# Values computed once, in pass 1, with the matmuls of the scores, in a gated cross-attention layer

## The chip, the cores and the metric

The kernel runs on one core of a Trainium2 chip. The metric is the device time of one execution in microseconds. Three runs of the kernel before gave 2297.72, 2296.51 and 2291.89 us; the median is 2296.51 us. Everything is in fp32.

## The reference

The layer takes tokens x (64 batches of 128 tokens with 512 features) and a context of the same shape. It has an attention part, whose score matrix is summed over all 64 batches, and a feed-forward part.

```
xn = layernorm(x)                                  # (64, 128, 512)
Q, K, V = xn, ctx, ctx, each head times Wh[h]      # 4 heads of 128
A = max(|sum over b of (Q K^T)[b] * decay / sqrt(128)|, 1)   # (4, 128, 128)
O = A V                                            # per batch and head
Y = layernorm(O, eps=1e-3) * gamma + beta
x = x + tanh(g_xattn) * ((relu(xn @ wg) * Y) @ wo)
x = x + tanh(g_ffn) * ffn(layernorm(x))            # SwiGLU, 512 -> 1408 -> 512
```

Because A needs the sum over all batches, no batch can be finished before all batches have gone through the scores. The kernel therefore makes two passes over the data. Q K^T is computed as (xn Wh Wh^T) ctx^T, so that K itself is never needed; V = ctx Wh is.

## The kernel before

The 64 batches are handled as 16 groups of 4 batches (512 tokens). On TensorE the stationary operand is a 128x128 block, the moving operand has 128 to 512 columns, and results go to PSUM. Three PSUM buffers (the pool `ps_mm`, L98) are shared by short-lived results: the transposes `pt`, the queries `pq`, the values `pv` and the attention outputs `po`. Five more PSUM tiles have fixed names (`bank_a`, `bank_f`, `bank_b`, `bank_c0`, `bank_c1`).

**Pass 1** loops over the groups. `prepare` (L407) normalises the tokens of a group on VectorE (statistics at L171, the normalisation at L199) and transposes them on TensorE (L178), with the copy out of PSUM on VectorE (L423) or ScalarE (L425) in turn. For the group before it, `scores` (L428) makes queries with four matmuls of 512 columns (L432, copied out by ScalarE at L436) and then, for each batch and head, one matmul of 128 columns with the context as stationary operand (L442). These accumulate over all batches and groups in `bank_c1`, so pass 1 writes no score out of PSUM. `project` (L452) computes relu(xn @ wg) by a Strassen-like scheme with seven products of four 256-column matmuls each (`product`, L202, matmul at L207), evacuated by ScalarE and VectorE, and stores the result in DRAM (`w_scr`, two stores a group on ScalarE's DMA queue, L482). Beside this, `prepare_weights` loads the raw FFN and output weights, forms their block sums on GpSimd and stores them in DRAM scratch (L367 loads, L391 stores), one part for each group.

**Between the passes**, the accumulated scores are multiplied by the decay mask on VectorE (L511), made absolute on ScalarE and raised to at least 1 on VectorE, which gives `attn`.

**Pass 2** loops over the groups again. `retention` (L527) loads nothing itself: it gets the four context tiles of the group, makes the values `v` with 16 matmuls of 128 columns (L534, four head blocks for each batch, copied out by ScalarE at L538), multiplies them by `attn` (L544), normalises and transposes the result (through DRAM, `sq_scr`, for all groups but the first), and multiplies it into the gate `w_t`, which was loaded from `w_scr` at L523. `attended` (L608) multiplies by wo and adds to the tokens. `ffn` (L732) then runs on the group with Strassen-like products against weights streamed from DRAM (`gu` at L723, `dn_w` at L729). The function `interleave` (L30) mixes the steps of `ffn` of one group with those of `attended` and `retention` of the next two by their announced numbers of steps (`RET_STEPS`, `ATT_STEPS`, `FFN_STEPS`).

What decides the order: every engine runs its own instructions in program order, and so does each DMA queue. The written order above is the start; the framework reorders it when the kernel is built and puts semaphore waits where a tile is reused or where a DMA takes over one of eight DMA semaphores (so that a DMA also waits for one issued some eight places before it, from whichever queue). SP's queue carries almost all loads: the tokens `x_t` (L110, five buffers of half a group each), the context `c_t` (L119, five buffers of one batch each), the weights, and the stores of `gu_scr` and `dn_scr`.

Of the kernel before, what the change touches and what calls it, by code (L numbers as in the profile page):

```python
# [10 lines left out]
F32 = mybir.dt.float32  # L11
# [30 lines left out]
def after(steps, gen):  # L42

    for _ in range(steps):
        yield
    yield from gen
# [3 lines left out]
def flamingo_gated_layer(  # L50
# [42 lines left out]
    xin = ctx.enter_context(tc.tile_pool(name="xin", bufs=5))  # L93
    cin = ctx.enter_context(tc.tile_pool(name="cin", bufs=5))
    att = ctx.enter_context(tc.tile_pool(name="att", bufs=1))
# [20 lines left out]

    def load_ctx(b):
        t = cin.tile([P, H, S], F32, tag="c", name="c_t")
        nc.sync.dma_start(out=t, in_=ctxT[b])  # L119
        return t  # L120

# [8 lines left out]
    attn = const.tile([P, H, S], F32, name="attn")  # L130
    wh_sb = const.tile([P, H, P], F32, name="wh_sb")
    gamma_sb = const.tile([P, NC], F32, name="gamma_sb")
# [13 lines left out]
    ]  # L146
    w_scr = dram.tile([NG, 2, P, 2, TOK], F32, name="w_scr")


# [5 lines left out]
    bank_c1 = ps_bank.tile([P, TOK], F32, name="bank_c1")  # L155
    for seeded in (bank_b, bank_c0):
        for i in range(TOK // P):
            nc.tensor.matmul(
                seeded[:, i * P : (i + 1) * P], lhsT=ident, rhs=ident,
                start=(i == 0), stop=True, skip_group_check=True,  # L160
            )
# [91 lines left out]
    pass1 = ExitStack()  # L253
    rows = pass1.enter_context(tc.tile_pool(name="rows", bufs=6))
    once = pass1.enter_context(tc.tile_pool(name="once", bufs=1))
# [11 lines left out]
    x_next.append(load_x(1))  # L267
    c_next = [load_ctx(b) for b in range(GB)]
    gates = const.tile([P, 2], F32, name="gates")
# [25 lines left out]
    def constants():  # L295

        nc.sync.dma_start(out=ds, in_=down_s.partition_broadcast(P))
        nc.sync.dma_start(out=decay, in_=decayT)
        nc.sync.dma_start(out=wh_sb, in_=wh.rearrange("h d e -> d h e"))
# [104 lines left out]

    acc = bank_c1.rearrange("p (h s) -> p h s", h=H)

    def prepare(g, x_t, xnT):  # L407
# [19 lines left out]

    def scores(g, c_t, xnT):  # L428
        qs = []
        for h in range(H):  # L430
            pq = ps_mm.tile([P, TOK], F32, tag="mm", name="pq")
            nc.tensor.matmul(  # L432
                pq, lhsT=gram[:, h, :], rhs=xnT[:, h, :], start=True, stop=True
            )
            q = rows.tile([P, TOK], F32, tag="row", name="q")
            nc.scalar.copy(q, pq)  # L436
            qs.append(q)
            if h % 2:
                yield
        for j in range(GB):  # L440
            for h in range(H):
                nc.tensor.matmul(  # L442
                    acc[:, h, :],
                    lhsT=c_t[j][:, h, :],
                    rhs=qs[h][:, j * S : (j + 1) * S],
                    start=(g == 0 and j == 0 and h == 0),
                    stop=(g == NG - 1 and j == GB - 1),
                    skip_group_check=True,
                )
            yield  # L450

    def project(g, xnT):  # L452
# [34 lines left out]
    for g in range(NG):  # L487
        x_t, c_t = x_next.pop(0), c_next
# [9 lines left out]
        interleave(  # L498
            (prep, GB),
            (scores(*pending) if pending else None, 2 + GB),  # L500
            (project(pending[0], pending[2]) if pending else None, 7),
        )
        x_next.append(load_x((g + 2) % NG))
        c_next = [load_ctx((g + 1) % NG * GB + j) for j in range(GB)]
        pending = (g, c_t, xnT)
    for _ in weights:
# [3 lines left out]

    nc.vector.tensor_mul(attn, acc, decay)  # L511
    absd = rows.tile([P, H, S], F32, tag="row", name="absd")
    nc.scalar.activation(absd, attn, AF.Abs)
# [12 lines left out]

    def retention(g, c_t, ws):  # L527

        helper = nc.vector if g < 3 else nc.gpsimd
        v = att.tile([P, H, GB, P], F32, tag="v", name="v")  # L530
        for j in range(GB):
            pv = ps_mm.tile([P, H, P], F32, tag="mm", name="pv")
            for h in range(H):
                nc.tensor.matmul(  # L534
                    pv[:, h, :], lhsT=c_t[j][:, h, :], rhs=wh_sb[:, h, :],
                    start=True, stop=True,
                )
            nc.scalar.copy(v[:, :, j, :], pv)  # L538
            yield

# [11 lines left out]
        if g:  # L552
            sq = att.tile([P, NQ, NC, GB, SQ], F32, tag="v", name="sq")
        ons = []
# [53 lines left out]
    def attended(g, x_t, ws, x1nT):  # L608
# [55 lines left out]
        if g:  # L664
            sq = att.tile([P, NQ, NC, GB, SQ], F32, tag="v", name="sq")
        for j in range(GB):
# [18 lines left out]
    WAIT = 5  # L685
    RET_STEPS = 8 + WAIT + 2
    ATT_STEPS = 8 + GB

    def new_x1nT():
        return wide.tile([P, NQ, NC, GB, SQ], F32, tag="xT", name="x1nT")  # L690

    x_t, c_t = x_next.pop(0), c_next
    c_next = [load_ctx(GB + j) for j in range(GB)]
    ws = load_gate(0)
    interleave(
        (retention(0, c_t, ws), 12), (after(6, project(pending[0], pending[2])), 16),
    )
# [219 lines left out]
    def next_retention(g):  # L917

        nonlocal c_next, ws
        c_t = c_next  # L920
        ws = load_gate(g)
        yield from retention(g, c_t, ws)
        if g + 1 < NG:
            c_next = [load_ctx((g + 1) * GB + j) for j in range(GB)]
# [6 lines left out]
    interleave((attended(0, x_t, ws, x1nT), ATT_STEPS), (islice(second, 7), 10))  # L931
    pending = (0, x_t, x1nT, combine_tokens(nc.vector, x1nT))
    for g in range(NG - 1):
# [6 lines left out]
        if g == 0:  # L940
            steps.append(late_attended(1, x_t, x1nT))
            n_steps += RET_STEPS - 7
        if g + 2 < NG:
# [64 lines left out]
```

## Time and profile before

The profiled execution took 2293.72 us; its span, from the first to the last instruction, is 2291.9 us. The TensorE clock was granted at 0.999.

| what | value |
|---|---|
| median of three runs | 2296.51 us |
| profiled execution / its span | 2293.72 / 2291.9 us |
| pass 1, last scores matmul | at 350 us |
| first FFN product | at 394.6 us |
| DMA, whole span | 459.17 MB, 200 GB/s |
| DMA share in pass 1, first slices | 0.8 and falling to 0.6 |
| context loads (L119) | 128 of 256 KB, 4.3 us to landing (median) |
| token loads in pass 1 (L110) | 512 KB, 5.4 us to landing (median), 3.8 to 9.6 |
| gate stores w_scr (L482) | 32 of 512 KB on ScalarE's queue, 0.34 us to issue |
| stores of FFN sums gu_scr (L391) | 7.3 to 11.3 us to landing, median 9.7 |

How to read it: a line of a group gives the line of the code, the engine, the operation with output and input tiles, the number of instructions, their busy time and mean duration, and the idle time of the engine just before them with what ended it. PEld is the load of stationary operands; it overlaps the matmuls (PE). "SPq" and "ACTq" are DMA issues on the queues of SP and ScalarE. Lines of a timeline begin with the start in the span and the time that the merged instructions took.

### The profile page before, as it was taken

The page shows a single profiled execution, that of the slowest core. Times are in us where ns is not written, and L with a number is a line of the kernel's source. Part 1 is how long each engine was busy: PE and PEld are TensorE (multiplying, and loading weights), DVE is VectorE, ACT ScalarE, POOL GpSimd, SP SyncE. Part 2 cuts the span into 40 slices and gives each one's busy share as a digit, 9 for nine tenths or more (in the row PEclk, how much of TensorE's full clock was granted, in tenths as well). Part 3 has the DMA queues.
Part 4 walks back from the last instruction along what each step waited for, and adds up shares of the span by engine and source line. Part 5 has one row for each costly group of instructions (what it writes and reads, how often), then busy time and mean ns, then how long its engine had stood idle before and what let it go on. Part 6 is the DMA issues. An engine that isn't in the chain of part 4 may idle for free. (4 is left out here: it accounts for less than half of the span.)

```text
span 2291.9 us, 28061 instructions
## 1 busy us (share of the span) xinstructions
PE 2263.7 (99%) x10808; PEld 1945.1 (85%) x10808; DVE 861.6 (38%) x1771; ACT 574.7 (25%) x1052; POOL 674.5 (29%) x811
## 2 busy tenths in 40 slices
PE   8999999999999999999999999999999999999999
PEld 7777787888888888888888888888888888888888
DVE  6444534544333333323333423343433333333222
ACT  2333333312222221213131212121222122222221
POOL 4232202322232323232424232423223242323210
PEclk9999999999999999999999999999999999999999
DMA  8777746566565656665666656565657475645541
GB/s 266 264 232 244 248 161 228 189 195 225 178 226 173 219 187 212 197 220 193 218 197 197 208 191 225 181 214 181 214 171 236 158 236 174 230 155 186 167 149 65
DMA packets 158213, 459.17 MB, mean 200 GB/s; under 512 B 16768, under 2 KB 36864, under 8 KB 143360
## 3 DMA queue, kind: packets, MB, share of 16 engines
q1 hardware_dynamic: 152656, 440.34, 58.9%
q10 hardware_dynamic: 5424, 17.04, 1.8%
q8 instruction: 85, 1.39, 0.3%
q14 instruction: 48, 0.39, 0.1%
HBM read 376.72 MB, written 80.61 MB: 200 GB/s over the span
## 5 line engine op out<-in xcount | busy, mean ns | idle before, releaser
L207 PE MATMUL bank_c<-tcomb,gu 128*128 128x256 f32 x1920 | 456.9, 379 | 1.0 <-ACT bank_b L766 0.7
L207 PEld LDWEIGHTS bank_c<-tcomb,gu 128*128 128x128 f32 x1920 | 361.3, 190 | 49.4 <-ACT bank_b L766 1.5
L207 PE MATMUL bank_a<-x1nT,gu 128*128 128x256 f32 x1280 | 302.8, 379 | 1.1 <-ACT x1nT L677 0.7
L207 PEld LDWEIGHTS bank_a<-x1nT,gu 128*128 128x128 f32 x1280 | 242.1, 190 | 34.5 <-ACT x1nT L677 1.2
L247 POOL TENSOR_TENSOR hs<-h,h 128x256 f32<-128x256 f32 x80 | 58.0, 726 | 582.7 <-DVE h L746 582.7
L167 POOL TENSOR_TENSOR rs<-ve,mhalf 128x1 f32<-128x1 f32 x128 | 72.6, 576 | 486.4 <-DVE ve L166 471.2
L745 ACT ACTIVATE sil<-c,gs_sb 128x256 f32<-128x256 f32 x160 | 81.2, 508 | 322.7 <-DVE c L775 183.2
L603 POOL TENSOR_TENSOR w_t<-w_t,yT 128x256 f32<-128x256 f32 x112 | 77.9, 726 | 264.2 <-ACT yT L594 264.2
L207 PE MATMUL bank_b<-x1nT,gu 128*128 128x256 f32 x640 | 151.7, 379 | 0.0
L207 PE MATMUL bank_f<-tcomb,gu 128*128 128x256 f32 x640 | 151.2, 379 | 0.0
L798 PE MATMUL bank_c<-dn_w,hs 128*128 128x256 f32 x640 | 145.0, 382 | 0.0
L775 DVE TENSOR_TENSOR c<-bank_c,m 128x512 f32<-128x512 f32 x80 | 55.0, 688 | 237.6 <-PE bank_c L207 234.2
L798 PE MATMUL bank_f<-dn_w,h 128*128 128x256 f32 x640 | 143.4, 379 | 0.0
L798 PEld LDWEIGHTS bank_f<-dn_w,h 128*128 128x128 f32 x640 | 121.5, 190 | 22.4 <-issue 6.7
L207 PEld LDWEIGHTS bank_b<-x1nT,gu 128*128 128x128 f32 x640 | 121.6, 190 | 22.1 <-issue 6.2
L798 PEld LDWEIGHTS bank_c<-dn_w,hs 128*128 128x128 f32 x640 | 120.3, 190 | 19.7 <-ACT bank_b L875 4.0
L207 PEld LDWEIGHTS bank_f<-tcomb,gu 128*128 128x128 f32 x640 | 121.6, 190 | 16.6
L746 DVE SCALAR_TENSOR_TENSOR h<-bank_a,us_sb,sil 128x256 f32<-128x256 f32 x80 | 38.6, 482 | 240.2 <-ACT sil L745 240.2
L171 DVE BATCH_NORM_STATS2 st<-x_t 128x6 f32<-128x512 f32 x128 | 83.0, 684 | 103.3 <-DMA x_t<-in_x_dram 102.2
L758 ACT COPY bank_c<-bank_a 128x512 f32<-128x512 f32 x80 | 45.6, 570 | 258.6 <-PE bank_a L207 256.8
L746 DVE SCALAR_TENSOR_TENSOR h<-c,us_sb,sil 128x256 f32<-128x256 f32 x160 | 78.3, 489 | 75.1 <-ACT sil L745 75.1
L207 PE MATMUL bank_c<-t,wgc 128*128 128x256 f32 x384 | 92.5, 383 | 0.0
(166 smaller groups left out, 3518.1 us busy)
## 6 DMA issues: line engine op xcount, KB each, us to landing
gu<-gu_scr SPq DMA_DIRECT2D x80, 1024.0 KB, 4.9
dn_w<-dn_scr SPq DMA_DIRECT2D x112, 640.0 KB, 5.1
gu<-gu_scr SPq DMA_DIRECT2D x80, 768.0 KB, 5.9
c_t<-in_ctxT_dram SPq DMA_DIRECT2D x128, 256.0 KB, 4.3
x_t<-in_x_dram SPq DMA_DIRECT2D x62, 512.0 KB, 4.6
sq_scr<-sq SPq DMA_DIRECT2D x30, 1024.0 KB, 4.8
wo_w<-wo_scr SPq DMA_DIRECT2D x112, 256.0 KB, 3.9
w_scr<-w ACTq DMA_DIRECT2D x32, 512.0 KB, 5.8
```

What stands on the lines that cost most here:

```text
L167: nc.gpsimd.tensor_tensor(dst, ve, mhalf[:, :n], ALU.pow)
L171: nc.vector.bn_stats(st, src)
L207: nc.tensor.matmul(out, lhsT=w[:, s, k, :], rhs=x_k, start=(start and s == 0 and k == 0), stop=(s == 1 and k == KC - 1), skip_group_check= ...
L247: engine.tensor_tensor(s[0], a21, a22, ALU.add)
L603: (helper if d else nc.gpsimd).tensor_tensor(w, w, yT[:, :, d * KC + k, q * 2 : q * 2 + 2, :], ALU.mult)
L745: nc.scalar.activation(sil, src[:, 0:n], AF.Silu, scale=gs_sb[:, i : i + 1])
L746: nc.vector.scalar_tensor_tensor(dst, src[:, n : 2 * n], us_sb[:, i : i + 1], sil, ALU.mult, ALU.mult)
L758: nc.scalar.copy(bank_c, bank_a)
L775: nc.vector.tensor_add(c22, bank_c, m5)
L798: nc.tensor.matmul(bank[:, i * HN : (i + 1) * HN], lhsT=lhs[:, j, i * P : (i + 1) * P], rhs=dn[:, j, :], start=(start and i == 0 and j == ...
```

## The change

The values are made in pass 1. For each context block (batch j, head h) one matmul now has 256 moving columns: 128 of queries and 128 of the head matrix Wh[h]. Both lie in one tile `qw` (five slots for each head: four batches of queries and Wh in the fifth), so the moving operand is two pieces of 128 columns with a step between them. Two batches share one PSUM tile `sv` of the pool `ps_mm`: the scores of both accumulate in its first part, the values go to the second and third. After each `sv` tile, VectorE adds the scores to `attn` in SBUF (the first time it copies them), and ScalarE copies the values into `v`. A group's `v` (1 MB) is stored in DRAM (`v_scr`) by ScalarE's queue, and pass 2 loads it back with one load on SP's queue in place of the four context loads. From the second group on, the context of pass 1 is loaded by ScalarE's queue, issued after the scores of the group before. Pass 2 no longer reads the context.

`bank_c1` no longer holds the scores and is seeded with the other banks at the start; the transposition buffer `sq` of pass 2 no longer shares its place with `v`; the pools of context and queries end with pass 1. `retention` is four steps shorter, and the first group's `project` starts three steps before `retention` does.

```diff
-    def load_ctx(b):
-        t = cin.tile([P, H, S], F32, tag="c", name="c_t")
-        nc.sync.dma_start(out=t, in_=ctxT[b])
-        return t
+    def load_ctx(g, engine):
+        tiles = []
+        for j in range(GB):
+            t = cin.tile([P, H, S], F32, tag="c", name="c_t")
+            engine.dma_start(out=t, in_=ctxT[g * GB + j])
+            tiles.append(t)
+        return tiles
...
-    for seeded in (bank_b, bank_c0):
+    for seeded in (bank_b, bank_c0, bank_c1):
...
+    qw = once.tile([P, H, GB + 1, P], F32, name="qw")
+    nc.sync.dma_start(out=qw[:, :, GB, :], in_=wh.rearrange("h d e -> d h e"))
...
-    def scores(g, c_t, xnT):
-        qs = []
+    def scores(g, xnT):
+        nonlocal c_next
+        c_t = c_next
         for h in range(H):
-            pq = ps_mm.tile([P, TOK], F32, tag="mm", name="pq")
+            pq = ps_mm.tile([P, GB, S], F32, tag="mm", name="pq")
             nc.tensor.matmul(
                 pq, lhsT=gram[:, h, :], rhs=xnT[:, h, :], start=True, stop=True
             )
-            q = rows.tile([P, TOK], F32, tag="row", name="q")
-            nc.scalar.copy(q, pq)
-            qs.append(q)
+            nc.scalar.copy(qw[:, h, 0:GB, :], pq)
             if h % 2:
                 yield
-        for j in range(GB):
-            for h in range(H):
-                nc.tensor.matmul(
-                    acc[:, h, :],
-                    lhsT=c_t[j][:, h, :],
-                    rhs=qs[h][:, j * S : (j + 1) * S],
-                    start=(g == 0 and j == 0 and h == 0),
-                    stop=(g == NG - 1 and j == GB - 1),
-                    skip_group_check=True,
-                )
-            yield
+        v = att.tile([P, H, GB, P], F32, tag="sq" if g % 2 else "v", name="v")
+        for h in range(H):
+            for q in range(2):
+                sv = ps_mm.tile([P, 4, P], F32, tag="mm", name="sv")
+                for i in range(2):
+                    j = 2 * q + i
+                    nc.tensor.matmul(
+                        sv[:, 0 : 2 + i : 1 + i, :],
+                        lhsT=c_t[j][:, h, :],
+                        rhs=qw[:, h, j : GB + 1 : GB - j, :],
+                        start=(i == 0),
+                        stop=(i == 1),
+                        skip_group_check=True,
+                    )
+                if g == 0 and q == 0:
+                    nc.vector.tensor_copy(attn[:, h, :], sv[:, 0, :])
+                else:
+                    nc.vector.tensor_add(attn[:, h, :], attn[:, h, :], sv[:, 0, :])
+                nc.scalar.copy(v[:, h, 2 * q : 2 * q + 2, :], sv[:, 1:3, :])
+            yield
+        nc.scalar.dma_start(out=v_scr[g], in_=v)
+        if g + 1 < NG:
+            c_next = load_ctx(g + 1, nc.scalar)
...
-    nc.vector.tensor_mul(attn, acc, decay)
+    nc.vector.tensor_mul(attn, attn, decay)
...
+    def load_values(g):
+        v = att.tile([P, H, GB, P], F32, tag="v", name="v")
+        nc.sync.dma_start(out=v, in_=v_scr[g])
+        return v
+
-    def retention(g, c_t, ws):
+    def retention(g, v, ws):
...
-        v = att.tile([P, H, GB, P], F32, tag="v", name="v")
-        for j in range(GB):
-            pv = ps_mm.tile([P, H, P], F32, tag="mm", name="pv")
-            for h in range(H):
-                nc.tensor.matmul(
-                    pv[:, h, :], lhsT=c_t[j][:, h, :], rhs=wh_sb[:, h, :],
-                    start=True, stop=True,
-                )
-            nc.scalar.copy(v[:, :, j, :], pv)
-            yield
...
-            sq = att.tile([P, NQ, NC, GB, SQ], F32, tag="v", name="sq")
+            sq = att.tile([P, NQ, NC, GB, SQ], F32, tag="sq", name="sq")
...
-    RET_STEPS = 8 + WAIT + 2
+    RET_STEPS = 4 + WAIT + 2
...
-        (retention(0, c_t, ws), 12), (after(6, project(pending[0], pending[2])), 16),
+        (after(3, retention(0, v, ws)), 11), (project(*pending), 9),
```

More of the change, by code (lines that the diff above doesn't have):

```diff
@@ L93, in flamingo_gated_layer @@
     xin = ctx.enter_context(tc.tile_pool(name="xin", bufs=5))
-    cin = ctx.enter_context(tc.tile_pool(name="cin", bufs=5))
     att = ctx.enter_context(tc.tile_pool(name="att", bufs=1))
@@ L130, in flamingo_gated_layer @@
     attn = const.tile([P, H, S], F32, name="attn")
-    wh_sb = const.tile([P, H, P], F32, name="wh_sb")
     gamma_sb = const.tile([P, NC], F32, name="gamma_sb")
@@ L147, in flamingo_gated_layer @@
     w_scr = dram.tile([NG, 2, P, 2, TOK], F32, name="w_scr")
+    v_scr = dram.tile([NG, P, H, GB, P], F32, name="v_scr")
     bank_a = ps_bank.tile([P, TOK], F32, name="bank_a")
@@ L253, in flamingo_gated_layer @@
     pass1 = ExitStack()
-    rows = pass1.enter_context(tc.tile_pool(name="rows", bufs=6))
+    cin = pass1.enter_context(tc.tile_pool(name="cin", bufs=5))
     once = pass1.enter_context(tc.tile_pool(name="once", bufs=1))
@@ L267, in flamingo_gated_layer @@
     x_next.append(load_x(1))
-    c_next = [load_ctx(b) for b in range(GB)]
+    c_next = load_ctx(0, nc.sync)
+    qw = once.tile([P, H, GB + 1, P], F32, name="qw")
+    nc.sync.dma_start(out=qw[:, :, GB, :], in_=wh.rearrange("h d e -> d h e"))
     gates = const.tile([P, 2], F32, name="gates")
@@ L298, in constants @@
         nc.sync.dma_start(out=decay, in_=decayT)
-        nc.sync.dma_start(out=wh_sb, in_=wh.rearrange("h d e -> d h e"))
         nc.sync.dma_start(out=gamma_sb, in_=gamma.rearrange("(c p) -> p c", p=P))
@@ L403, in rest_weights @@
         )
-    acc = bank_c1.rearrange("p (h s) -> p h s", h=H)
     def prepare(g, x_t, xnT):
@@ L487, in flamingo_gated_layer @@
     for g in range(NG):
-        x_t, c_t = x_next.pop(0), c_next
+        x_t = x_next.pop(0)
         xnT = wide.tile([P, NC, TOK], F32, tag="xT", name="xnT")
@@ L499, in flamingo_gated_layer @@
             (prep, GB),
-            (scores(*pending) if pending else None, 2 + GB),
-            (project(pending[0], pending[2]) if pending else None, 7),
+            (scores(*pending) if pending else None, 2 + H),
+            (project(*pending) if pending else None, 7),
         )
         x_next.append(load_x((g + 2) % NG))
-        c_next = [load_ctx((g + 1) % NG * GB + j) for j in range(GB)]
-        pending = (g, c_t, xnT)
+        pending = (g, xnT)
     for _ in weights:
@@ L508, in flamingo_gated_layer @@
     interleave((scores(*pending), 1))
-    nc.vector.tensor_mul(attn, acc, decay)
-    absd = rows.tile([P, H, S], F32, tag="row", name="absd")
+    nc.vector.tensor_mul(attn, attn, decay)
+    absd = once.tile([P, H, S], F32, tag="m5p", name="absd")
     nc.scalar.activation(absd, attn, AF.Abs)
@@ L664, in attended @@
         if g:
-            sq = att.tile([P, NQ, NC, GB, SQ], F32, tag="v", name="sq")
+            sq = att.tile([P, NQ, NC, GB, SQ], F32, tag="sq", name="sq")
         for j in range(GB):
@@ L690, in new_x1nT @@
         return wide.tile([P, NQ, NC, GB, SQ], F32, tag="xT", name="x1nT")
-    x_t, c_t = x_next.pop(0), c_next
-    c_next = [load_ctx(GB + j) for j in range(GB)]
+    x_t = x_next.pop(0)
+    v = load_values(0)
     ws = load_gate(0)
     interleave(
-        (retention(0, c_t, ws), 12), (after(6, project(pending[0], pending[2])), 16),
+        (after(3, retention(0, v, ws)), 11), (project(*pending), 9),
     )
@@ L917, in next_retention @@
     def next_retention(g):
-        nonlocal c_next, ws
-        c_t = c_next
+        nonlocal ws
+        v = load_values(g)
         ws = load_gate(g)
-        yield from retention(g, c_t, ws)
-        if g + 1 < NG:
-            c_next = [load_ctx((g + 1) * GB + j) for j in range(GB)]
+        yield from retention(g, v, ws)
     def late_attended(g, x_t, x1nT):
@@ L930, in flamingo_gated_layer @@
     second = next_retention(1)
-    interleave((attended(0, x_t, ws, x1nT), ATT_STEPS), (islice(second, 7), 10))
+    interleave((attended(0, x_t, ws, x1nT), ATT_STEPS), (islice(second, 4), 8))
     pending = (0, x_t, x1nT, combine_tokens(nc.vector, x1nT))
@@ L941, in flamingo_gated_layer @@
             steps.append(late_attended(1, x_t, x1nT))
-            n_steps += RET_STEPS - 7
+            n_steps += RET_STEPS - 4
         if g + 2 < NG:
```

## The prediction

> **What bounds the kernel now.** I read part 1 of the page first, then the busy time by stage, then single groups in order of time.
>
> ```profile
> PE 2263.7 (99%) x10808; PEld 1945.1 (85%) x10808; DVE 861.6 (38%) x1771; ACT 574.7 (25%) x1052; POOL 674.5 (29%) x811
> ```
>
> TensorE is the bound. The stage table (span; then busy time of PE, PEld, DVE, ACT, POOL; clock; DMA share; GB/s) shows where it still waits:
>
> ```profile
> 100.00:200.00 100.00, 96.47 (x507) 78.66 (x506) 47.94 (x102) 34.77 (x57) 27.06 (x25) 1.00 0.72 245
> 200.00:300.00 100.00, 95.10 (x518) 79.27 (x517) 44.01 (x91) 32.03 (x52) 21.60 (x19) 1.00 0.68 229
> 600.00:700.00 100.00, 100.00 (x464) 87.07 (x463) 36.48 (x78) 21.41 (x40) 34.63 (x43) 1.00 0.62 203
> ```
>
> Pass 2 is solid matmul; pass 1 (to about 350 us) loses 4 to 5%. Two groups of instructions are touched by the change, and one shows the waits of pass 1 (last field: idle time before, by releaser):
>
> ```profile
> L534 PE MATMUL pv<-wh_sb,c_t 128*128 128x128 f32 x512 | 67.5, 275 | 0.0
> L442 PE MATMUL bank_c<-q,c_t 128*128 128x128 f32 x512 | 67.3, 275 | 0.0
> L432 PE MATMUL pq<-xnT,gram 128*128 128x512 f32 x128 | 62.0, 608 | 12.3 <-DVE xnT L423 9.4 <-DVE mean_var L172 2.9
> ```
>
> Each fp32 matmul is two passes (256 matmuls, x512). Their 275 ns overlap, so the pace must be read from starts. One group of pass 1, TensorE:
>
> ```profile
> 102.13 1.89 PE L207 MATMUL bank_a<-xnT,wgc 128*128 128x256 f32 x8
> ...
> 120.45 1.06 PE L442 MATMUL bank_c<-q,c_t 128*128 128x128 f32 x8
> 121.34 1.89 PE L207 MATMUL bank_c<-t,wgc 128*128 128x256 f32 x8
> 123.07 1.89 PE L207 MATMUL bank_a<-xnT,wgc 128*128 128x256 f32 x8
> 127.32 1.10 PE L432 MATMUL pq<-xnT,gram 128*128 128x512 f32 x2 [2.36 <-DVE xnT L423]
> ```
>
> A pass of 128 columns takes 0.89/8 = 0.111 us, one of 256 takes 1.73/8 = 0.216 us; a group takes 123.07 - 102.13 = 20.94 us. The 2.36 us stall is explained by SP's queue and VectorE in the same group:
>
> ```profile
> 103.38 0.96 SPq L391 DMA_DIRECT2D gu_scr<-gu_raw  x2
> 113.89 1.92 SPq L367 DMA_DIRECT2D gu_raw<-in_gateT_dram  x4
> ...
> 118.44 0.41 SPq L110 DMA_DIRECT2D x_t<-in_x_dram  x1
> ```
>
> ```profile
> 124.50 1.29 DVE L171 BATCH_NORM_STATS2 st<-x_t 128x6 f32<-128x512 f32 x2 [6.14 <-DMA x_t<-in_x_dram]
> ```
>
> Five groups out of sixteen look like this: the raw FFN weights wait until the last store of sums has landed, the tokens queue behind them, and VectorE, which runs in order, stands 6.14 us at the statistics. Today little hangs on VectorE at that point.
>
> **The arithmetic on TensorE.** Removed: 512 + 512 passes of 128 columns, 1024 x 0.111 = 113.7 us. Added: 256 matmuls of 256 columns, 512 x 0.216 = 110.6 us. Gain 3.1 us. The strided moving operand is charged nothing: products on x1nT, cut into 4x2x32, also run at 379 ns a pass. Here the Trainium skill would promise more. "TensorE: Matmul & The Clock Gate", section "LDWEIGHTS (loading the stationary operand)", gives a load of 128 columns as columns/1.2 ns, 107 ns, and the change saves 512 loads: 55 us if they stood in the way. The pace of 0.111 us a pass with a load in each says that they overlap the streaming, so I take 3.1. The eight seeding matmuls of bank_c1 lie in the wait for the first tokens: nothing.
>
> Work moves, too: a group of pass 1 grows from 20.94 to 20.94 - 32 x 0.111 + 32 x 0.216 = 24.3 us, and pass 2 loses 3.6 us a group.
>
> **Pass 2.** Four context loads of 256 KB become one v load of 1 MB, 4.9 us to landing by the gu row of that size. In the built order it is issued as soon as the previous group's po matmuls have read v, a whole FFN ahead (119 us between like products of two groups), so it costs nothing; so do the ScalarE copies that go (ACT is 21% busy). With sq in a buffer of its own nothing waits for v longer.
>
> **What pass 1 gets: 8 evacuations a group.** Each sv tile needs a VectorE addition of 128x128 (estimate 0.38 us, from 0.48 at 256 and 0.69 at 512 elements) and then a ScalarE copy of 128x256 (0.47 us, what L745 takes from bank_c). In the built order the copy waits for the addition, and TensorE's tile three further on waits for the copy (three PSUM buffers, shared with pq and pt). The busy time is covered: 8 x 0.38 = 3 us and 8 x 0.47 = 3.8 us in 24 us on engines that are half idle or more. What is not covered is standing in line. I count from G, the start of a group's first product on TensorE: product 1.73, two pq 1.72, pt 0.44, product 1.73, half product 0.86, two pq 1.72, half product 0.86, pt 0.44 make 9.5; two sv tiles 11.2; product 12.95; two sv 14.7; product 16.4; pt and one sv 17.7. The next sv needs the buffer of the tile finished at 14.7. But the built order of VectorE puts the two statistics of the next tokens between the additions of the two tiles finished before 14.7. So tokens not landed by about 15.4 stop TensorE at 17.7.
>
> When do they land? Their load waits for the normalisation that frees the buffer: 9.5 + copy 0.69 + normalise 0.54 = 10.8, and landing takes 5.4 (median of pass 1): 16.3. Then statistics 1.29, addition 0.38, copy 0.47, hand-overs 0.1: 18.5, so 0.8 us late. Nine ordinary groups: +7 us (0 at the shortest landing of 3.8, 15 at one a us longer).
>
> In the five groups with FFN sums the load comes at 118.44 - 102.13 = 16.3 even today. The v store adds 1 MB to the burst in front of it (x 0.5, w_scr 1, sums 1.75 MB moved from 102.9 to 113.8, 313 GB/s), 3.4 us; one context load less in between, -0.4. Issue 19.3, landing after 5.5 at 24.8, +2.2 = 27.0: 9.3 us late; without any delay by v, 5.9. I take 8: 5 x 8 = 40, less the 9.4 us that the pq row loses today, +31 us (20 to 45).
>
> **Context loads and v stores on ScalarE's queue.** Issue: 7 a group instead of 2 at 0.34 us (w_scr row), +1.7 us a group on ScalarE, covered. Waits: in the built order every load waits for a DMA some eight places earlier, whoever issued it. In five groups, the last context load waits for the v store issued just before it, and behind it on ScalarE stand the copy of bank_a, four q copies and an xnT copy, for which TensorE waits. The v store goes out at G + 1.0 (relu 0.6, issue 0.34) and lands 4.8 us later (row sq_scr, 1 MB) to 9 (the w_scr store issued at 104 held its reader until 113). I take 6.5: G + 7.5, issue and copy 0.9: 8.4, where TensorE wants it at 5.6: 2.8 us, five times: +14 us (5 to 25).
>
> The other side is SP, which is rid of this:
>
> ```profile
> SPq L119 <- PE bank_c L442: 115.7, 44, 11.2
> SPq L367 <- DMA gu_scr<-gu_raw: 40.4, 5, 10.6
> ```
>
> The 115.7 us are waits of context loads with tokens behind them. But the tokens then wait for VectorE, or in the five groups for the second row, which stays. The rule against the move: "DMA: Bandwidth & Descriptors", section "Issuing engines are not separate DMA queues", says that copies from any engine share the same 16 DMA engines. If ScalarE's queue were bandwidth of its own, the 3.4 us of v above would fall away (-17 us over five groups); by the 313 GB/s burst, above what any slice of the page averages (266), I side with the rule.
>
> **The turn from pass 1 to pass 2.** From 350 to 395 us TensorE already stands some 6 us, on the chain po, statistics, transposes, gating, ys. The eight pv tiles (7.1 us) that filled parts of it are gone, and group 1's v load waits for group 0's last po, with the first FFN weights behind it on SP (issued at 374 today for a product at 395: covered). Products are moved forward to cover the attn chain (3.5 us over about 2.6). Between 0 (all stalls elsewhere) and 9; I take +5.
>
> **Sum.** -3 + 7 + 31 + 14 + 5 = +54 on the span of 2291.9: 2346. The profiled execution took 2293.72, 1.8 more, and the median of the runs is 2.8 above that: 2350 us. Stalls at one place give time to the next, so I shade to 2345.
>
> **Rivals.** *SP freed (2284 us).* With no context loads ahead of them, tokens land before G + 15.4 everywhere; the 9.4 us of waits vanish and the 3.1 us count. It decides if the landing drops below 4.5 us and the weights no longer hold the queue. For it: the 115.7. Against: the buffers and the 40.4.
> *Covered (2298 us).* VectorE's wait is late by less than the three PSUM buffers hold, ScalarE's v store lands within 4.5 us; stalls stay at 12 us and the turn takes the 3. For it: DVE has idled 6 us before with 2.4 us lost. Against: the additions now behind that idle time.
> *DMA saturated (2395 us).* 16 MB more pass through pass 1; bursts overlap, context tiles come late as well, and every group loses 5 to 6 us: 16 x 6 = 96. Against: per time the mean load hardly rises, as a group is 3.4 us longer.
>
> **Numbers.** Main case 0.67 (2312 to 2380), SP freed 0.10, covered 0.10, saturated 0.13. Within 0.3% (2289.6 to 2303.4) is what a measurement cannot tell from no change: faster 0.10, same 0.10, slower 0.80. The range 2302 to 2385 leaves out SP freed, part of covered and the top of saturated.
>
> **What would show it.** The stage table: PE busy in pass 1 near 90% and pass 1 ending at about 455 us instead of 350 (53 from longer groups, 52 from stalls), pass 2 still 100% and 3.6 us a group shorter. The sv groups carry idle time with releaser ACT v; VectorE's statistics 6 to 10 us waits on x_t in five groups; ScalarE's context loads wait on v_scr. Wrong: idle time on sv under 10 us, or TensorE waiting for v in pass 2, or a 256-column pass above 0.216.

## The result and the profile after

The changed kernel took 2369.49 us (median of 4 runs, 2368.97 to 2372.05); the kernel before, beside it, 2296.74 us (4 runs, 2291.89 to 2297.72). The ratio is 1.0323, 95% interval 1.0305 to 1.0341: slower by 73 us. The profiled execution has a span of 2367.4 us (before 2291.9) and a mean granted TensorE clock of 0.988.

Part 1 of the page after, busy time by engine:

```profile
PE 2288.1 (97%) x10304; PEld 1936.9 (82%) x10304; DVE 905.5 (38%) x1899; ACT 585.5 (25%) x1116; POOL 671.0 (28%) x811
```

TensorE has 504 recorded passes fewer, and yet 24 us more of busy time. The stage table (same columns as before) says where:

```profile
100.00:200.00 100.00, 86.06 (x359) 67.58 (x358) 39.65 (x93) 31.82 (x64) 19.36 (x19) 0.91 0.57 196
200.00:300.00 100.00, 82.00 (x350) 65.07 (x348) 39.48 (x94) 29.91 (x60) 20.30 (x18) 0.91 0.62 217
600.00:700.00 100.00, 99.78 (x456) 86.06 (x455) 44.54 (x89) 21.27 (x39) 27.33 (x35) 1.00 0.68 225
```

In pass 1 TensorE is busy 82 to 86% of the time, where it was 95 to 96%, and its clock is granted at 0.91. The DMA share fell, from 0.72 and 0.68 to 0.57 and 0.62, so the transfers are not what fills the time (e2 will show the same bytes passing faster). Pass 2 looks as before at this scale. The groups show what TensorE waited for:

```profile
L450 PE MATMUL sv<-qw,c_t 128*128 128x256 f32 x512 | 129.6, 398 | 26.5 <-ACT qw L440 22.0 <-ACT w L483 3.2 <-ACT v L462 1.2
L209 PE MATMUL bank_a<-xnT,wgc 128*128 128x256 f32 x256 | 68.0, 401 | 28.6 <-ACT bank_c L477 28.6
L437 PE MATMUL pq<-xnT,gram 128*128 128x512 f32 x128 | 67.0, 650 | 0.3 <-DVE xnT L425 0.3
```

The 9.4 us that pq lost to VectorE before are gone. In their place stand 28.6 us before bank_a and 26.5 us before sv, nearly all released by copies of ScalarE. These copies are short; ScalarE itself was late. Its waits in pass 1 that end at a DMA, or at an issue (us in total, times, longest):

```profile
ACT qw L440 <- DMA c_t<-in_ctxT_dram: 30.0, 4, 8.1
ACT bank_c L477 <- issue: 26.7, 3, 9.6
...
ACT bank_c L477 <- DMA dn_scr<-dn_t: 16.1, 2, 8.3
...
ACT bank_c L477 <- DMA c_t<-in_ctxT_dram: 11.9, 1, 11.9
```

These are 84.7 us in ten waits. (ScalarE also waited 79.0 us for VectorE's additions before it copied values, but in 106 short waits, and TensorE waited only 1.2 us for those copies.) A copy from PSUM to PSUM or SBUF needs no DMA. What waits is a DMA issue in front of it in ScalarE's program.

In what follows, a *dn group* is one of the five groups of pass 1 in which sums of the FFN's down weights are stored (dn_scr), a *gu group* one of the five with sums of its gate and up weights (gu_scr); one group more stores those of the output weights (wo_scr). The *partner* of a DMA is the one that used its semaphore before it. One dn group, in order of time:

```profile
100.85 3.03 SPq L395 DMA_DIRECT2D dn_scr<-dn_raw  x3
...
103.99 4.25 SPq L395 DMA_DIRECT2D dn_scr<-dn_t  x4
104.01 1.88 PE L437 MATMUL pq<-xnT,gram 128*128 128x512 f32 x4
...
106.16 1.89 PE L209 MATMUL bank_f<-t,wgc 128*128 128x256 f32 x8
...
110.30 0.36 ACTq L498 DMA_DIRECT2D w_scr<-w  x1
110.69 1.09 ACTq L120 DMA_DIRECT2D c_t<-in_ctxT_dram  x2
111.83 0.57 ACT L477 COPY bank_c<-bank_a 128x512 f32<-128x512 f32 x1 [8.75 <-issue]
...
112.45 1.51 PE L209 MATMUL bank_a<-xnT,wgc 128*128 128x256 f32 x4 [4.40 <-ACT bank_c L477]
...
113.76 3.23 PE L437 MATMUL pq<-xnT,gram 128*128 128x512 f32 x4
```

The gate store at 110.30 had its data at 103. In the built order its partner is a dn_scr store of SP, eight places before it. The trace, which records the semaphore and the landing of every DMA, agrees: the last of the three dn_scr stores from 100.85 on, issued at 102.16, had this semaphore before, and it landed at 110.22. The first context load behind it had a dn_scr store as partner too; that landed at 110.56, and the load went out at 110.69. ScalarE stands for 8.75 us, TensorE for 4.40. The last line shows the second price: four pq passes took 1.88 us at 104.01 and 3.23 us at 113.76, since after the wait the clock was granted at half (0.50 in the columns of the stage table):

```profile
113.06:116.47 3.41, 3.41 (x7) 1.67 (x6) 0.00 (x0) 1.90 (x4) 2.18 (x3) 0.50 1.02 380
```

In four of the gu groups the same happens with a context load whose partner is a context load too. In one of them the partner was issued at 136.09 and landed at 146.99, and the next load went out at 147.01:

```profile
134.99 2.23 ACTq L120 DMA_DIRECT2D c_t<-in_ctxT_dram  x2
...
141.88 0.60 PE L180 MATMUL pt<-ident,xn 128*128 128x128 f32 x4
...
147.01 0.33 ACTq L120 DMA_DIRECT2D c_t<-in_ctxT_dram  x1
147.38 1.07 ACT L440 COPY qw<-pq 128x512 f32<-128x512 f32 x2 [7.58 <-DMA c_t<-in_ctxT_dram]
...
148.02 3.78 PE L450 MATMUL sv<-qw,c_t 128*128 128x256 f32 x8 [5.54 <-ACT qw L440]
```

All ten long waits of ScalarE end like this: the DMA that held it went out within 0.1 us of the landing of its partner. In the five dn groups that is the gate store, behind a dn_scr store; in the group with wo_scr stores it is the gate store and three context loads, one after the other; in four gu groups it is a context load behind a context load.

**Where the 75.5 us of span went.** From the starts of TensorE's passes in each trace I took the distance to the next start, less the pace of that pass (the median distance: 0.112, 0.216 and 0.429 us for 128, 256 and 512 columns, 0.109 for a transpose). The first column is the sum of the paces, called work from here on; the others are what exceeds them, the stalls. The turn is the stretch from the last scores to the first FFN product.

| us | work | until 20 us | pass 1 | turn | pass 2 | half-clock passes in these |
|---|---|---|---|---|---|---|
| before | 2249.2 | 7.7 | 12.1 | 6.6 | 8.1 | 1.4 |
| after | 2246.0 | 7.0 | 80.8 | 8.2 | 17.5 | 19.0 |

Work fell by 3.2 and the start by 0.7; pass 1 lost 68.7 more, the turn 1.6, pass 2 9.4. Of after's 80.8 us, twelve stalls over 0.9 us make 56.7 (six before bank_a 29.6, six before sv 27.1), and passes that ran at half clock make 19.0. Ten of the twelve, 52.2 us, lie behind ScalarE's ten waits; the other two (1.4 and 3.1 us) stand behind a copy of values and a Relu.

### The profile page after: what moved, and what is told of

It reads as the page before. It is cut to its first block, busy times and chain, and to the rows that moved or that the text cites. A ratio compares the mean times of both kernels' runs of the same rounds, so it can differ in the third digit from the quotient of the medians.

```text
span 2367.4 us, 27227 instructions
## 1 busy us (share of the span) xinstructions
PE 2288.1 (97%) x10304; PEld 1936.9 (82%) x10304; DVE 905.5 (38%) x1899; ACT 585.5 (25%) x1116; POOL 671.0 (28%) x811
## 4 chain that ended last, share of the span: by engine, by line
PE 87%; DMA 6%; DVE 4%; POOL 1%; issue 1%; ACTq 1%; ACT 0%; SPq 0%; DVEq 0%; POOLq 0%
PE bank_c L209 19%; PE bank_a L209 12%; PE bank_c L808 9%; PE bank_f L209 6%; PE bank_f L808 6%; PE bank_b L209 6%; PE sv L450 4%; PE by L632 3%; PE bank_b L808 3%; PE bank_a L808 3%; PE bx L632 2%; PE po L554 2%; PE bz L632 2%; DMA c_t<-in_ctxT_dram 2%; PE bank_c L822 2%; PE pq L437 1%
## 5 line engine op out<-in xcount | busy, mean ns | idle before, releaser
L450 PE MATMUL sv<-qw,c_t 128*128 128x256 f32 x512 | 129.6, 398 | 26.5 <-ACT qw L440 22.0
L450 PEld LDWEIGHTS sv<-qw,c_t 128*128 128x128 f32 x512 | 97.6, 199 | 42.1 <-ACT qw L440 23.2
L643 POOL TENSOR_TENSOR x_t<-x_t,m 128x512 f32<-128x512 f32 x48 | 62.8, 1335 | 162.8 <-ACT m L649 150.9
```

Source lines behind the costliest of these rows:

```text
L450: nc.tensor.matmul(sv[:, 0 : 2 + i : 1 + i, :], lhsT=c_t[j][:, h, :], rhs=qw[:, h, j : GB + 1 : GB - j, :], start=(i == 0), stop=(i == 1), ...
L643: engine.tensor_tensor(dst, dst, src.rearrange("p (b d) -> p b d", b=2), ALU.add)
```

## The experiments

Eleven kernels, in three batches. The kernel before, run beside them, had medians of 2292.32 us (first four), 2293.48 (e5 to e8) and 2292.55 us (e9 to e11). Changing one line may change the whole built order of pass 1, so no experiment moves one wait alone; each is read with its trace.

### e1 and e2: context loads, then the value stores too, on SP's queue

```diff
-            c_next = load_ctx(g + 1, nc.scalar)
+            c_next = load_ctx(g + 1, nc.sync)
```

> The changed kernel with the context loads of pass 1 on SP's queue again; the v stores stay on ScalarE's. Theory (ScalarE, which runs in order, is stopped by the DMA waits in front of its context loads and stores, and TensorE then waits for its copies and loses clock): most of the 80.8 us of waits of pass 1 go, but in the built order the second gate store still waits on ScalarE for a context load issued on SP just before, so some 1 us a group stays: 2300 to 2320 us, granted clock above 0.995. Rival 1 (the 16 MB of v stores crowd the DMA engines in pass 1): bytes are the same, 2355 to 2375 us. Rival 2 (my prediction's main term: statistics of late tokens stand between the additions on VectorE): 2340 us or more, with idle time on sv whose releaser is ScalarE's copy of v.

Measured 2333.65 us, ratio 1.0180 (1.0163 to 1.0198). Some 44% of the loss is gone, and the time is above what was expected. Pass 1 still has 44.1 us of stalls (before 12.1), pass 2 17.6 (before 8.1; see e6). More than half of those of pass 1 are another stall, in the five gu groups. Timeline of e1:

```profile
198.43 1.92 SPq L371 DMA_DIRECT2D gu_raw<-in_gateT_dram  x4
...
200.39 2.00 SPq L371 DMA_DIRECT2D gu_raw<-in_upT_dram  x4
...
202.49 0.41 SPq L109 DMA_DIRECT2D x_t<-in_x_dram  x1
...
206.83 1.29 DVE L173 BATCH_NORM_STATS2 st<-x_t 128x6 f32<-128x512 f32 x2 [7.32 <-DMA x_t<-in_x_dram]
...
209.42 0.27 DVE L461 TENSOR_TENSOR attn<-attn,sv 128x128 f32<-128x128 f32 x1
209.73 0.77 ACT L462 COPY v<-sv 128x256 f32<-128x256 f32 x2 [7.74 <-DVE attn L461]
...
210.15 3.35 PE L450 MATMUL sv<-qw,c_t 128*128 128x256 f32 x7 [4.89 <-ACT v L462]
```

Tokens queued behind raw weights, statistics, addition, value copy, TensorE: this is the chain that the prediction wrote down for these groups. Its stalls in the five are 5.9, 4.9, 5.1, 2.2 and 5.7 us, 23.8 in all; half clock comes on top.

```diff
-        nc.scalar.dma_start(out=v_scr[g], in_=v)
+        nc.sync.dma_start(out=v_scr[g], in_=v)
...
-            c_next = load_ctx(g + 1, nc.scalar)
+            c_next = load_ctx(g + 1, nc.sync)
```

> The changed kernel with the context loads and the v stores on SP's queue; ScalarE issues only the two gate stores of a group, as before the change. Theory (DMA waits on ScalarE): the waits of pass 1 fall to what the kernel before had, some 12 us, and only the 3 us of matmuls less, the turn and pass 2 count: 2290 to 2304 us, clock 0.998 or more. Rival 1 (DMA bytes): 2355 to 2375 us. Rival 2 (VectorE's statistics): 2340 us or more.

Measured 2302.13 us, ratio 1.0040 (1.0026 to 1.0053). With every byte of the change still moved, some 87% of the loss is gone, so bandwidth was not its cause. Stages of e2:

```profile
100.00:200.00 100.00, 98.07 (x450) 78.74 (x450) 49.34 (x116) 40.76 (x81) 24.92 (x24) 1.00 0.73 253
200.00:300.00 100.00, 96.82 (x442) 77.39 (x441) 49.30 (x116) 39.35 (x79) 25.07 (x24) 1.00 0.70 250
```

The same bytes pass in less time at 250 GB/s, and the clock is whole. VectorE waits for tokens nearly as long as before the change (94.9 us in 25 waits):

```profile
DVE st L173 <- DMA x_t<-in_x_dram: 85.2, 23, 6.2
```

but the built order has the token load of a gu group ahead of the raw weights (at 183.28 in one of them, the weights from 184.84), and TensorE loses only 8.6 us to value copies in nine waits of at most 2.3. That three PSUM buffers bridge the rest of VectorE's waits is my reading of the order; no run tests it.

### e3: the kernel before, with its context loads on ScalarE's queue

```diff
-        c_next = [load_ctx((g + 1) % NG * GB + j) for j in range(GB)]
+        c_next = [load_ctx((g + 1) % NG * GB + j, nc.scalar) for j in range(GB)]
```

> The kernel before, with only the context loads of its pass 1 on ScalarE's queue. No values are made in pass 1 and no bytes are added. Theory (DMA waits on ScalarE): slower than before by 20 to 60 us, with TensorE idle for ScalarE's copies and a granted clock below 0.995. Rivals 1 and 2 (bytes, VectorE): within 5 us of before, 2292 to 2302 us.

(`load_ctx` takes the queue as an argument here.) Measured 2304.66 us, ratio 1.0051 (1.0036 to 1.0066): slower by 12 us, less than expected, and not for the reason expected. Stalls in pass 1 rose from 12.1 to 24.4 us (some 7 to 9 of it half clock), the long ones now before bank_c products. One of them:

```profile
170.73 0.69 DVE L171 BATCH_NORM_STATS2 st<-x_t 128x6 f32<-128x512 f32 x1 [12.19 <-DMA x_t<-in_x_dram]
171.34 0.67 DVE L473 TENSOR_TENSOR w<-bank_c,m5p 128x512 f32<-128x512 f32 x1
...
172.07 2.19 PE L207 MATMUL bank_c<-t,wgc 128*128 128x256 f32 x5 [4.99 <-DVE w L473]
```

VectorE stood 12.19 us at the statistics of late tokens, and the addition that frees bank_c stood behind them. ScalarE did wait for context loads (16.7 us in six waits), but TensorE was not held by it. The moved loads alone, without value stores and additions per tile, do not bring about the stalls of the changed kernel.

### e4 and e10: 256 columns as two of 128

```diff
-                    nc.tensor.matmul(
-                        sv[:, 0 : 2 + i : 1 + i, :],
-                        lhsT=c_t[j][:, h, :],
-                        rhs=qw[:, h, j : GB + 1 : GB - j, :],
-                        start=(i == 0),
-                        stop=(i == 1),
-                        skip_group_check=True,
-                    )
+                    for dst, slot in ((0, j), (1 + i, GB)):
+                        nc.tensor.matmul(
+                            sv[:, dst, :],
+                            lhsT=c_t[j][:, h, :],
+                            rhs=qw[:, h, slot, :],
+                            start=(i == 0 and dst == 0),
+                            stop=(i == 1 and dst > 0),
+                            skip_group_check=True,
+                        )
```

In e4 this is done to the changed kernel, in e10 to e8 (below), where no wait of pass 1 covers it.

> The changed kernel with each matmul of 256 moving columns cut into two of 128 (queries, then the head matrix) into the same places: 256 more loads of the stationary operand. If the load is hidden behind the streaming, as the pace of 0.111 us a pass says, 3 to 4 us of TensorE work come back, less what falls into waits: 2369 to 2374 us. If loads stood in the way, 512 passes more at up to 0.107 us: 2400 us or more.

> e8_all_sp with each score matmul of 256 moving columns as two of 128: what the wide form is worth where no wait of pass 1 covers it. The split adds 512 passes of 0.1115 us less what 512 of 0.216 lose: 512 x (2 x 0.1115 - 0.216) = 3.6 us for the pairs of passes counted once, and 7 us as the work column of e4_split_128 had it (380.0 against 373.1): 2281.8 + 4 to 7 = 2285-2289. If the wide form is worth nothing, 2282; if loads of stationary tiles get in the way of the short passes, over 2292.

e4: 2377.38 us, ratio 1.0371 (1.0353 to 1.0389), 8 us over the changed kernel by the medians and 11 by the ratios, and above the expected range. e10: 2286.97 us, ratio 0.9974 (0.9966 to 0.9982), 5 to 6 us over e8, as expected. (The 0.107 us in the expectation of e4 is the figure that the prediction cites.) In both traces a pass of the split matmuls keeps the pace of 0.112 us, with a load in each. The split is thus 512 x (2 x 0.112 - 0.216) = 4.1 us of work; the rest is stalls. The wide form is worth a few microseconds, and the 512 loads more come nowhere near 55 us.

### e5: only the value stores on SP's queue

The first of the two lines of e2 alone.

> The changed kernel with only the store of the values moved to SP's queue; context loads and gate stores stay on ScalarE's. It is the fourth of the four placings (both on ScalarE 2369.5, context moved alone 2333.7, both moved 2302.1). If the two parts simply add up, the store is worth 2333.7 - 2302.1 = 31.6 us here too: 2338. If what counts is which DMA stands eight places before a ScalarE DMA, the store on SP shifts those pairs, and in the built order the context loads of the groups with gu_scr stores then follow x_t loads and not the context load issued just before: the 27 us of stalls between transposes and score matmuls go with most of their clock loss, and the time falls below the sum, to 2305-2330. If the context loads alone carry the cost, 2355-2370.

Measured 2328.02 us, ratio 1.0149 (1.0133 to 1.0165), inside the range expected if the partners decide (2305 to 2330) and below the plain sum of the parts (2338). Pass 1 loses 37.2 us; no stall before bank_a is left, and the longest are sv matmuls that wait for the context itself (13.9 us in six waits) or for value copies.

### e7: one context load a group on ScalarE in place of four

```diff
-        tiles = []
-        for j in range(GB):
-            t = cin.tile([P, H, S], F32, tag="c", name="c_t")
-            engine.dma_start(out=t, in_=ctxT[g * GB + j])
-            tiles.append(t)
-        return tiles
+        t = cin.tile([P, GB, H, S], F32, tag="c", name="c_t")
+        engine.dma_start(
+            out=t, in_=ctxT[g * GB : (g + 1) * GB].rearrange("b d h s -> d b h s")
+        )
+        return [t[:, j] for j in range(GB)]
...
-    cin = pass1.enter_context(tc.tile_pool(name="cin", bufs=5))
+    cin = pass1.enter_context(tc.tile_pool(name="cin", bufs=1))
```

> The changed kernel with one context load of 1 MB for a group, in one buffer, in place of four of 256 KB in five; all still on ScalarE's queue, the same bytes. Theory (a DMA on ScalarE waits for the one eight places before it, and all of ScalarE's computing behind it): with three DMAs fewer a group the partners lie further back. In the built order no ScalarE DMA in a group with gu_scr stores then waits for a context load just issued, so the 27 us before the score matmuls go with their share of the clock loss; in the groups with dn_scr stores a gate store still waits for a dn_scr store and the value store for the context load, so about half of the 30 us there stays: 2315-2345. Rival, the bytes on the DMA engines at that point, or ScalarE's queue as such: no change, 2360-2372. A late context (one buffer, loaded only once the group's scores are done) would show as score matmuls waiting for c_t and could take it above.

Measured 2352.63 us, ratio 1.0251 (1.0229 to 1.0273): better than the changed kernel, but short of the expected range. The stalls of 5 to 6 us behind the q copies did go, as expected, though score matmuls now wait 11.7 us for value copies and 6.0 for the context itself. The six stalls before bank_a all stayed (7.5 us in the group with wo_scr stores, 3.2 to 4.4 in the dn groups). In the dn groups the partner of the value store is now the 1 MB context load issued some 9 us before it:

```profile
ACT bank_c L476 <- DMA c_t<-in_ctxT_dram: 39.6, 5, 8.6
```

Fewer DMAs change who is whose partner; they do not remove the waits.

### e11: the sums' stores issued by GpSimd

```diff
-                nc.sync.dma_start(out=dst, in_=src)
+                nc.gpsimd.dma_start(out=dst, in_=src)
```

> The changed kernel with the stores of the FFN and attention weight sums issued by GpSimd in place of SP; the three kinds of ScalarE DMA stay where the change put them. In the built order no ScalarE DMA then waits for a dn_scr or gu_scr store: those of the dn groups wait for x_t loads and weight loads of the group before. Theory (ScalarE stops because the DMA eight places before it is a store that is itself waiting for GpSimd's sums): the six stalls between bank_f and bank_a, 29.6 us, go, and about 8 us of clock loss with them; the ones before the score matmuls stay or shrink: 2315-2340. Rival (ScalarE's own three kinds of DMA are the price wherever the others come from): 2360-2372. GpSimd may issue its stores slowly and let its sums slip, which would show as late gu_raw and dn_raw loads, not as ScalarE waits.

Measured 2340.41 us, ratio 1.0208 (1.0192 to 1.0225): the total is just above what was expected (2315 to 2340), and the place is another one. The stalls before the sv matmuls shrank to 5.5 us. The six before bank_a stayed, 26.2 us, but ScalarE's waits behind them name another DMA:

```profile
ACT bank_c L477 <- DMA gu_raw<-in_gateT_dram: 44.1, 5, 9.4
```

The dn_scr stores are gone from ScalarE's waits. In the gu groups the partners of a gate store, and in one group of a context load, are now raw weight loads, and in each group the gate store went out within 0.1 us of its partner's landing. Which DMA holds ScalarE follows the order of the issues; that only stores waiting for GpSimd's sums are long enough to hurt is refuted.

### e6: the old spacing in pass 2

On e2:

```diff
-            (ffn(*pending), FFN_STEPS), (chain(*steps), int(n_steps * 1.05)),
+            (ffn(*pending), FFN_STEPS), (chain(*steps), int((n_steps + 4) * 1.05)),
```

> The version with context loads and value stores on SP, and pass 2's interleaving stretched as before the change: the factor is applied to four steps more, so that the steps of attention lie at the old places between the FFN's steps. Theory: the 9.4 us that pass 2 lost are 13 times one 0.377 us wait of TensorE (its first matmul on bank_c after the one on bank_b waits for VectorE's addition that reads bank_c, which stands behind the statistics of an attention step) and smaller ones on the same path, made by the new step positions. It goes: 2302.1 - 9.4 = 2293, level with before (2292.3). If the loss belongs to the loads of values instead of context or to the removed matmuls, it stays at 2300-2304; if another pair of steps collides instead, anywhere from 2293 to 2310.

Measured 2293.62 us, ratio 0.9998 (0.9990 to 1.0006). Pass 2's stalls went from 17.5 to 9.2 us. What they had been, from e2's timeline of one group:

```profile
1081.43 0.70 DVE L185 STREAM_TRANSPOSE sq<-xn 128x512 f32<-128x512 f32 x1
1082.06 0.65 DVE L785 TENSOR_TENSOR c<-bank_c,m 128x512 f32<-128x512 f32 x1
...
1082.77 1.99 PE L209 MATMUL bank_c<-tcomb,gu 128*128 128x256 f32 x8 [0.21 <-DVE c L785]
```

The addition that frees bank_c stands behind the statistics, normalisation and transposition of an attention step, and TensorE loses 0.377 us from start to start (the idle field, 0.21, is measured from the modelled end). It is there in all 13 groups of the steady stretch, with 0.3 us of smaller ones. In e6 these waits of bank_c for the addition are gone. Taking four steps out of the count had shifted that step onto this addition.

### e8 and e9: no DMA on ScalarE at all in pass 1

e8 is e6 with the gate stores on SP's queue too; e9 is the kernel before with the same edit and nothing else.

```diff
-            nc.scalar.dma_start(out=w_scr[g, q], in_=w[:, q])
+            nc.sync.dma_start(out=w_scr[g, q], in_=w[:, q])
```

> The version of e6_spacing with the gate stores on SP's queue too, so that ScalarE issues no DMA in pass 1 at all. If ScalarE's remaining gate stores still cost TensorE something (12.8 us of stalls are left in pass 1, as many as before the change), 2285-2292, under both kernels; if they no longer cost, level with e6_spacing, 2291-2295; if the gate stores, queued on SP behind sums and loads, land late and the next group's Relu into the same single buffer waits for them, 2300-2330.

> The kernel before with its gate stores on SP's queue, so that ScalarE issues no DMA in pass 1 there either. It tells what of e8_all_sp's 11.7 us belongs to the change and what to the gate stores. The stalls of before in pass 1 (12.1 us) end at VectorE's copy of the transposed tokens (9.4 us in five waits), which waits for tokens loaded late behind the weights, not at ScalarE. If that cause is right, the gate stores cost before nothing: 2290-2296. If ScalarE's gate stores held the same 10 us there, 2281-2286, and the change itself would be worth nothing even when freed.

e8: 2281.79 us, ratio 0.9949 (0.9937 to 0.9962). e9: 2282.79 us, ratio 0.9958 (0.9944 to 0.9972). Both beat both kernels of the study; e8 is below its expected range, and e9 in the range that I had given to the other answer. Stages of e8, then of e9:

```profile
100.00:200.00 100.00, 100.00 (x467) 82.25 (x466) 54.38 (x123) 42.82 (x83) 25.93 (x24) 1.00 0.74 262
200.00:300.00 100.00, 100.00 (x465) 82.22 (x464) 52.31 (x123) 42.80 (x83) 28.38 (x26) 1.00 0.76 263
```

```profile
100.00:200.00 100.00, 100.00 (x534) 82.62 (x533) 51.22 (x98) 35.66 (x59) 26.73 (x25) 1.00 0.79 260
200.00:300.00 100.00, 100.00 (x531) 82.50 (x530) 50.95 (x94) 35.82 (x58) 21.91 (x19) 1.00 0.70 231
```

Pass 1 is solid matmul in both: 1.3 and 2.2 us of stalls from 20 us to its end. e9 went against my expectation. I had put its 9.4 us of waits down to VectorE and its late tokens, and expected nothing from the gate stores. With them on SP's queue, VectorE waits less for tokens (before, then e9):

```profile
DVE st L171 <- DMA x_t<-in_x_dram: 94.9, 25, 7.3
```

```profile
DVE st L171 <- DMA x_t<-in_x_dram: 50.4, 23, 4.3
```

In e8 the fall is larger: 10.1 us in 5 waits, where e6 has 83.6 in 23, and TensorE's waits for value copies in pass 1 go from 7.1 to 0.2 us. This agrees with the reading that TensorE stood behind VectorE's waits for tokens; that the gate stores had no part in those was wrong. The gain is not the freeing of ScalarE either. In the kernel before, ScalarE waited for gate stores only 7.6 us, in three waits, and TensorE's waits in pass 1 all end at VectorE. In one of the gu groups before, the token load was issued at 207.74 for queries that TensorE would have reached at 212.8 (216.34, when it began them, less the stall of 3.5); in e9 at 199.65 for queries at 205.74, one microsecond earlier in the group. The raw weights in front of the tokens wait for the gu_scr stores, and these landed sooner: 9.4 us after their issue at the longest, 11.3 before. Why they did, and whether the order of SP's queue helped besides, these runs do not separate.

Set beside each other, e8 and e9 say what the change itself is worth with its queues mended: 0.9949 against 0.9958, with intervals that overlap. No gain can be told. The traces agree: e8's work is 2246.0 us and its stalls 25.4, e9's 2249.3 and 22.5. In this one pair of traces the 3.2 us saved on TensorE are given back in pass 2 (9.3 against 7.9) and at the start (7.3 against 5.5); the start alone lies between 5.5 and 9.3 in the traces, so its share is uncertain.

## Why the prediction was right, and where its working failed

The direction held, and the time fell inside the range: 2345 us predicted, 2369.5 measured, pass 1 ending at 474 us for the 455 announced. But the main term, late tokens in front of VectorE's additions, did not appear, and a small one was four times as large. That the sum came near is luck.

**TensorE's arithmetic: right.** -3.1 us predicted, -3.2 in the work column. The match is a little closer than it should be: with the pace of 0.112 us in place of 0.111 the exchange gives -4.1 (which e4 and e10 put back), and the eight passes that seed bank_c1, taken as nothing, add 0.9. The wide passes run at 0.216 us, as charged. The weight-load rule of the Trainium skill ("TensorE: Matmul & The Clock Gate", section "LDWEIGHTS (loading the stationary operand)") gives 55 us, by the prediction's estimate, for 512 loads saved if they stood in the way; the pace with a load in each pass shows that they do not.

**ScalarE stopped by its own DMA issues: right in kind, mis-sized.** The term was +14 us, from one pair (the last context load behind the value store) in five groups. I had seen that every DMA waits for one some eight places before it, and costed only the one pair that I found in the built order. What held TensorE were two other pairs, one in each kind of group: the gate store behind a dn_scr store, and a context load behind a context load (with the like in the group of the wo_scr stores). The stalls behind them were 52.2 us of 56.7, and e2 took nearly all of them away. The pair that I had costed held ScalarE by itself for 3.6 us, once.

**Late tokens, +7 and +31: the chain is real, but not in this kernel.** The page after has, for VectorE and for TensorE:

```profile
DVE st L173 <- DMA x_t<-in_x_dram: 18.9, 19, 2.9
```

```profile
PE sv L450 <- ACT v L462: 1.2, 1, 1.2
```

The waits for tokens fell (94.9 us before), but not because the tokens came early: in one gu group they were issued at 212.60, behind the raw weights, 15.5 us after the group's first product at 197.07. But TensorE had been held 5.1 us for the q copies in that group, and by 218.16, when the statistics ran without a wait, it had not yet come to an sv tile that needed them. e1, where ScalarE waits less, shows the predicted chain in the five groups at 60% of the size: 23.8 us for the 40 that stood behind the 31 (40 less the 9.4 that pq lost). The two stalls are alternatives at one place, and I added them; shading 2350 to 2345 was far too little for that. (Two small slips in the ordinary groups change nothing: 10.8 + 5.4 is 16.2, and nine times 1.8 is 16.)

**Not foreseen: the clock, 17.6 us more, and pass 2, 9.4 us.** No term of the sum was a half clock, although stalls of some 3 and 8 us were in it. "Pass 2 costs nothing" looked at loads and buffers only; I had read the interleaving factors in the diff as bookkeeping, and e6 showed that a shift of the steps costs 0.4 us a group at one place, with smaller waits besides.

**The turn: +5 predicted, +1.6 measured**, inside its bounds.

**Rivals.** *DMA saturated* is refuted by the stage table (share down) and by e2. *SP freed* did not happen: the raw weights, with the tokens behind them, waited longer than before for the gu_scr stores (48.1 us in five waits, 40.4 before), and the waits of the context loads moved to a queue whose engine computes. *Covered* (2298 us) comes nearest to what e2 is, 2302 us.

**The signs announced.** PE near 90%: it was 82 to 86%. sv idle behind ACT v: 1.2 us; the releasers were ACT qw and ACT bank_c. Statistics 6 to 10 us late: no, at most 2.9. ScalarE's loads behind v_scr: 3.6 us, a minor part. Of the signs of being wrong none showed as worded: sv had 26.5 us of idle time, though with another releaser, no long wait of TensorE for v in pass 2 is in the trace, and the wide pass stayed at 0.216 us. Idle time alone was too weak a sign; its releaser is what told the mechanisms apart.

## What to carry to other kernels

A DMA issued by an engine that computes can hold that engine until its partner has landed, from whichever queue the partner came, and with it everything behind the issue (here 84.7 us in ten waits); look up the partners of every such DMA in the built order, in each kind of iteration, before moving one. When two late things stop the same engine at the same place, take the later one and not the sum, and expect the second to appear when the first is mended. And before crediting a change, mend the same fault in the kernel before: moving the gate stores was worth 11.8 us on the changed kernel (e6 to e8) and 9.8 us on the kernel before (e9).

## What the hardware showed that was not expected

The price of a stall of TensorE is more than the stall. In the thirteen traces a clock of 0.5, for 3.4 or 6.8 us (once 10.2), came with every stall of 3.9 us or more (39 of 39): it began during the stall or within 2 us of its end. Between 2.0 and 3.8 us it was 16 of 36, and of 29 stalls from 1.3 to 2.0 us one alone, of 1.6 us. Apart from the end of the program only one window, in e6, stands outside this count, after a 1.5 us stall and several shorter ones. The Trainium skill's rule ("TensorE: Matmul & The Clock Gate", section "HAM oscillation — how this bites in real kernels") warns of idle gaps over about 3.4 us; the trace agrees in size, without a sharp edge. In the changed kernel ten such windows in pass 1 cost 19.0 us on 56.7 us of long stalls; in e2, without the stalls, 1.3 us, at the start.
